# A two-layer decoder on one core: first rows loaded first, Mamba's weights laid out by a process, and another table of allowances for the order of work

## The chip, the cores and the metric

The kernel runs on one core of a Trainium2 chip. The core has four compute engines that run side by side, each through its own list of instructions in a fixed order: PE (TensorE, matrix products; PEld is its weight load), DVE (VectorE), ACT (ScalarE) and POOL (GpSimd). A fifth, SP (SyncE), issues all transfers between main memory and the core. The metric is the device time of one execution in microseconds (us), as the median of three runs.

## The reference, cut to what matters

The input `x` has 128 sequences of 64 rows of 128 numbers. Six layers follow one another, each added to `x`. All numbers are 32-bit floats unless said otherwise.

```python
x = x + mamba_block(layernorm(x))              # W_in, causal conv, scan over 64 steps, gate, W_out, then an MLP 128-512-128
x = x + pointer_attention(layernorm(x), ctx)   # each row looks at 3 rows of ctx named by an index; two softmaxes
x = x + bitlinear_ffn(layernorm(x))            # ternary weights, 8-bit activations, gelu, 128-512-128
x = x + causal_attention_twice(layernorm(x))   # 16 heads of 8; the context goes through a conv and becomes the next query
x = x + cross_attention(layernorm(x), ctx)     # 16 heads of 8, additive mask
x = x + moe(layernorm(x))                      # 8 experts 128-256-128, two best per row, all eight computed
# moe returns its own input as well: out = x_flat + sum_e cw[:, e] * (relu(x_flat @ W1[e] + b1[e]) @ W2[e] + b2[e])
```

In the Mamba block the input goes through `rmsnorm(., norm1_w)` and `W_in`; the time step is `softplus(... + dt_bias)`, the decay is `exp(-exp(A_log) * dt)`. The weights that multiply a normalized row (`norm1_w`, `norm2_w`, `norm_gate_w`) can be multiplied into the rows of `W_in`, `mlp_w1` and `W_out` once; the kernel does that.

## The kernel before, in words

The 128 sequences are worked in 16 groups of 8 (512 rows, held as 4 chunks of 128 rows). Each group passes through ten stages, named in `LAYERS`: prepare, project, recur, mlp (together the Mamba block), pointers, ternary, first, second (the two causal attentions), cross, experts. A stage takes one group at a time and seven groups are under way at once, since there are seven buffers for the rows (`x`). When the experts of a group are done, its rows are stored, its buffer is given back, and the rows of the group seven places later are loaded into it (`way`, L1718 to L1730).

What comes next on each engine is not decided on the chip. Each stage is written as a Python generator that says which engine it wants next and for how long (`yield V, 0.75`), or which token it needs (a buffer, a PSUM bank `"a"`, the four-bank tile `"s"`, its turn in a layer). The class `Turns` (L78) plays all generators against each other with these lengths before the program is built, and the order in which it serves them is the order of the instructions on PE, DVE, ACT and POOL. `dv`, `ac` and `po` (L369 to L376) are the lengths of elementwise work on DVE, ACT and POOL by the number of columns. Transfers on SP have no lengths there: a stage that needs one waits a fixed time (`yield None, 2.5` after the load of the rows), or none. The plan also halves PE's rate for a stretch of 3.413 us whose predecessor was less than 74% busy (`STRETCH`, `ENOUGH`).

Where several processes ask for one engine, the one that holds a scarce token goes first, and among equals the older one. The age is a tuple: the rank, then the time at which it asked plus the allowance of its layer (`age`, L142). A positive allowance makes a layer look younger, so it gives way. All processes have rank 0 but one: `ahead` (L1732), which turns the context rows of all groups into keys and values, has rank 1 and comes last always. The allowances are searched for while the program is built: `planned` (L228) tries 150 random changes of them, plays the plan with the instructions switched off (`Engine`, `Stand`), and keeps what ends earliest in the plan's own account.

The work ahead of the first group is not part of the plan. The parameter vectors are loaded and turned (L342 to L348), then `mamba` (L446) loads `W_in` (`win`), the conv weights, `W_out` (`wout`), `mlp_w1`, `mlp_w2` and the rest, and multiplies the norms into them on DVE (L454, L470, L472), each instruction in place in the lists as written. Only then does `way` issue the loads of the rows. A process `weights` (L1748) prepares the weights of the other layers among the work of the first groups.

Lines that the text below speaks of: L285 is every matrix product, L396 every transpose through PE, L398 the ACT copy behind it; L386 and L387 are the mean and variance of the rows on DVE, L365 and L366 the reciprocal root on POOL, L404 the centred rows `u` on POOL; L542 is the logarithm in prepare on ACT, L651 the last step of the decays on DVE; L1142 is the rounding of the hidden rows on POOL in the ternary layer; L1265 and L1267 are the maximum (`amx`, DVE) and its subtraction (POOL) in the cross attention; L1700 adds an expert's output to the rows on DVE.

## Time and profile before

| | |
|---|---|
| median of 3 runs | 2204.68 us (2203.23 to 2210.49) |
| profiled execution, its own time | 2200.66 us |
| its span, first to last instruction | 2198.8 us |
| mean clock granted to TensorE | 0.935 |
| PE busy | 1906.6 us, 87% of the span |
| DVE, ACT, POOL busy | 1474.3, 1163.1, 1005.9 us (67%, 53%, 46%) |
| DMA | 120.75 MB, mean 55 GB/s |

Busy times of PE are sums of matrix products as the profiler records them; a product takes longer where the granted clock is lower. "Idle before" a group of instructions is the time in which its engine had nothing running just before them, with the event that ended it, the releaser. A wait of an engine that is not the limit costs nothing by itself. The queries used are the page of the whole execution, the table of busy times by stretch, the list of waits by engine, the chain of work that ended last, and the timeline.

### The profile page before, as it was taken

The page shows a single profiled execution, that of the slowest core. Times are in us where ns is not written, and L with a number is a line of the kernel's source. Part 1 is how long each engine was busy: PE and PEld are TensorE (multiplying, and loading weights), DVE is VectorE, ACT ScalarE, POOL GpSimd, SP SyncE. Part 2 cuts the span into 40 slices and gives each one's busy share as a digit, 9 for nine tenths or more (in the row PEclk, how much of TensorE's full clock was granted, in tenths as well). Part 3 has the DMA queues.
Part 4 walks back from the last instruction along what each step waited for, and adds up shares of the span by engine and source line. Part 5 has one row for each costly group of instructions (what it writes and reads, how often), then busy time and mean ns, then how long its engine had stood idle before and what let it go on. Part 6 is the DMA issues. An engine that isn't in the chain of part 4 may idle for free.

```text
span 2198.8 us, 57057 instructions
## 1 busy us (share of the span) xinstructions
PE 1906.6 (87%) x23915; PEld 1352.6 (62%) x23920; DVE 1474.3 (67%) x3991; ACT 1163.1 (53%) x2134; POOL 1005.9 (46%) x1258
## 2 busy tenths in 40 slices
PE   3787678899998898989998989789988889898996
PEld 2555455566666566667666666566665666675664
DVE  2677777875576776767776876688586856745453
ACT  1555456655545654655554655556455545554442
POOL 1555755754426644363445462536453733523221
PEclk9888789999999999999999999889999999999998
DMA  6441212211112111021210201121101010101000
GB/s 179 160 151 56 73 40 79 80 50 35 38 63 81 64 52 59 25 68 38 86 35 21 97 33 56 55 83 38 45 18 61 14 41 2 35 7 41 26 6 6
DMA packets 87277, 120.75 MB, mean 55 GB/s; under 512 B 31622, under 2 KB 61292, under 8 KB 87020
## 3 DMA queue, kind: packets, MB, share of 16 engines
q1 hardware_dynamic: 87020, 117.10, 16.0%
q8 instruction: 188, 3.08, 0.6%
q14 instruction: 69, 0.57, 0.1%
HBM read 75.00 MB, written 42.07 MB: 53 GB/s over the span
## 4 chain that ended last, share of the span: by engine, by line
PE 52%; DVE 25%; POOL 9%; ACT 7%; DMA 3%; issue 3%; SPq 1%; DVEq 0%; POOLq 0%; ACTq 0%
PE psa L285 37%; PE pss L285 11%; PE psa L396 4%; POOL u L404 3%; DVE tops L1310 3%; DVE pT L1253 1%; DVE amx L1265 1%; DVE pT L609 1%; DVE st L386 1%; DMA x<-in_x 1%; DVE x L1700 1%; DVE sel L909 1%; DVE mv L387 1%; DVE s L916 1%; POOL r L1142 1%
## 5 line engine op out<-in xcount | busy, mean ns | idle before, releaser
L365 POOL TENSOR_SCALAR rsq<-mv 128x4 f32<-128x4 f32 x96 | 21.6, 225 | 538.9 <-DVE mv L387 532.2
L404 POOL TENSOR_SCALAR u<-x,mv,rstd 128x128 f32<-128x128 f32 x320 | 256.1, 811 | 23.2 <-PE psa L396 12.9
L285 PE MATMUL psa<-fT,moe_w 128*128 128x512 f32 x512 | 255.3, 615 | 10.2 <-DVE pT L651 3.7
L285 PEld LDWEIGHTS psa<-moe_w,hid 128*128 128x128 f32 x2048 | 244.4, 195 | 29.6 <-issue 19.8
L285 PE MATMUL psa<-moe_w,hid 128*128 128x128 f32 x2048 | 252.9, 279 | 4.1 <-ACT v_a L289 2.5
L1700 DVE SCALAR_TENSOR_TENSOR x<-psa,cw,x 128x128 f32<-128x128 f32 x512 | 144.0, 343 | 164.8 <-PE psa L285 164.8
L1678 ACT ACTIVATE hid<-psa,vcol 128x512 f32<-128x512 f32 x256 | 174.2, 688 | 150.3 <-PE psa L285 146.8
L1267 POOL TENSOR_TENSOR pT<-pT,amx 128x512 f32<-128x512 f32 x128 | 133.9, 1048 | 175.9 <-DVE amx L1265 151.6
L1343 ACT ACTIVATE pT<-pss 128x512 f32<-128x512 f32 x256 | 137.3, 604 | 104.4 <-PE pss L285 104.2
L1310 DVE TENSOR_REDUCE tops<-pss 128x32 f32<-128x2048 f32 x64 | 146.2, 2284 | 34.4 <-PE pss L285 34.2
L1142 POOL TENSOR_SCALAR r<-h 128x512 bf16<-128x512 f32 x64 | 98.3, 1544 | 143.6 <-DVE h L1140 106.7
L285 PEld LDWEIGHTS psa<-fT,moe_w 128*128 128x128 f32 x512 | 87.5, 192 | 83.8 <-issue 51.2
L285 PEld LDWEIGHTS pss<-km,qm 32*128 32x128 f32 x3072 | 103.1, 201 | 57.2 <-issue 39.8
L285 PE MATMUL pss<-km,qm 32*128 32x128 f32 x3072 | 122.5, 300 | 14.7 <-DVE pT L1253 8.6
L398 ACT COPY fT<-psa 128x512 f32<-128x512 f32 x112 | 65.8, 590 | 105.2 <-PE psa L396 105.0
L386 DVE BATCH_NORM_STATS2 st<-x 128x6 f32<-128x128 f32 x384 | 102.9, 268 | 24.4 <-DMA x<-in_x 23.8
L1387 DVE TENSOR_TENSOR fT<-psa,inv 128x256 f32<-128x256 f32 x96 | 40.2, 419 | 116.4 <-ACT inv L1385 114.2
L285 PE MATMUL psa<-pT,cst 128*32 128x256 f32 x1536 | 113.0, 404 | 3.8 <-DVE u L735 1.5
L1269 ACT ACTIVATE pT<-pT 128x512 f32<-128x512 f32 x128 | 79.8, 632 | 68.5 <-POOL pT L1267 68.0
L1383 ACT ACTIVATE inv<-psa 128x256 f32<-128x256 f32 x96 | 36.9, 384 | 120.5 <-PE psa L285 120.3
L396 PE MATMUL psa<-cst,u 128*128 128x128 f32 x384 | 72.9, 299 | 30.6 <-POOL u L404 22.9
L1253 DVE TENSOR_TENSOR pT<-pss,mask 128x512 f32<-128x512 f32 x128 | 87.3, 682 | 15.3 <-PE pss L285 15.2
(285 smaller groups left out, 4529.7 us busy)
## 6 DMA issues: line engine op xcount, KB each, us to landing
v_x<-v_x SPq DMA_DIRECT2D x32, 768.0 KB, 4.1
kT<-kT SPq DMA_DIRECT2D x32, 512.0 KB, 3.0
vo<-vo SPq DMA_DIRECT2D x32, 512.0 KB, 4.3
pT<-steps SPq DMA_DIRECT2D x64, 256.0 KB, 3.8
km<-km SPq DMA_DIRECT2D x32, 512.0 KB, 3.2
x<-in_x SPq DMA_DIRECT2D x16, 256.0 KB, 3.2
ctxT<-in_ctx SPq DMA_DIRECT2D x16, 256.0 KB, 2.7
mask<-in_mask_Bx1xSxS_ff SPq DMA_DIRECT2D x32, 128.0 KB, 2.8
```

Source lines behind the costliest of these rows:

```text
L285: T.matmul(o, lhsT=lhsT, rhs=rhs, start=start, stop=stop)
L386: V.bn_stats(st[:, c, :], X[:, c, :])
L396: T.transpose(pt[:, c * P : (c + 1) * P], part, by)
L404: G.tensor_scalar(u[:, c, :], X[:, c, :], mean(c), scale[:, c : c + 1], ALU.subtract, ALU.mult)
L1142: G.tensor_scalar(r2, h[:, c, :], -MAGIC, None, ALU.add)
L1253: V.tensor_tensor(sco, banks[:, r].rearrange("p (b h s) -> p b h s", b=4, s=S), mask[:, 4 * quad : 4 * quad + 4, :].unsqueeze(2).to_broadc ...
L1267: G.tensor_tensor(s3, s3, mx.unsqueeze(2).to_broadcast([P, 8, S]), ALU.subtract)
L1269: A.activation(sco, sco, AF.Exp)
L1310: V.tensor_reduce(mx[:, :, 0:8], banks.rearrange("p r (n s) -> p r n s", s=S), AX.X, ALU.max)
L1343: A.activation(pTs[r].rearrange("p b g q -> p (b g q)"), banks[:, r, :], AF.Exp)
L1678: A.activation(hid[:, b, :], ph, AF.Relu, bias=vec["moe_b1"][:, 2 * e + b : 2 * e + b + 1])
L1700: V.scalar_tensor_tensor(X[:, c, :], po_[:, c * P : (c + 1) * P], cw[:, c, e : e + 1], X[:, c, :], ALU.mult, ALU.add,)
```

## The change

The sum of all work stays the same: the same instructions of each kind on each engine, except that one load of an ACT table at the very start goes away. What changes is their order, in six ways.

1. The rows of group 0 are loaded right behind the constants, ahead of the parameter vectors and all weights.
2. What lays out Mamba's weights (multiplying the norms in, the decay constant, the identity for the scan) becomes a process of the plan, `setup`, with lengths. Two tokens, `win` and `wout`, hold prepare and recur back until it is done. The loads of the small parameters go ahead of `wout`, `mlp_w1` and `mlp_w2`.
3. The plan's length of POOL work becomes 0.22 + n/480 us for n columns (it was 0.1 + n/500), and the rounding of L1142 gets 1.55 us (it was 1.12).
4. The rank goes away. `ahead` is a process like the others with an allowance of 47.6 us.
5. The allowances are a table in the file in place of the search. The classes for playing the plan without instructions go away.
6. The small buffer `amx` has eight copies instead of four.

```diff
-    def layer(self, name):
-        self.running["allowance"] = self.allowances.get(name, 0.0)
+    def layer(self, name, group=None):
+        self.running["allowance"] = self.allowances.get(name, 0.0) + self.allowances.get((name, group), 0.0)
...
-        return process["rank"], process["time"] + process["allowance"], self.n
+        return process["time"] + process["allowance"], self.n
...
-def planned(layers, names, rounds=150):
...
+ALLOWANCES = {
+    "ahead": 47.6,
+    "mlp": 17.6,
+    "cross": -0.7,
+    "pointers": 12.3,
+    "ternary": -46.6,
+    "first": -6.5,
+    "second": 10.0,
+    "experts": 1.7,
+}
...
     def po(n):
-        return 0.1 + n / 500
+        return 0.22 + n / 480
...
         win = load("win", [P, 548], w["L0_attn_W_in"], mp)
-        V.tensor_scalar(win, win, vec["norm1_w"], None, ALU.mult)
+        dtb = broadcast(mp, "dt_bias", w["L0_attn_dt_bias"], 4)
+        alog = broadcast(mp, "A_log", w["L0_attn_A_log"], 4)
...
+        def setup():
+
+            yield None, 4.0
+            yield V, 1.2
+            V.tensor_scalar(win, win, vec["norm1_w"], None, ALU.mult)
+            for i in range(2):
+                V.tensor_copy(wbc[:, 32 * i : 32 * i + 16], win[:, 512 + 16 * i : 528 + 16 * i])
+            yield A, 0.2
+            A.activation(nega, alog, AF.Exp)
+            yield V, 0.8
+            V.tensor_scalar(nega, nega, -1.0, None, ALU.mult)
+            V.tensor_copy(eye4, ident.unsqueeze(1).to_broadcast([P, 4, P]))
+            turns.give("win")
+            yield None, 6.0
+            yield V, 0.5
+            for b in range(2):
+                V.tensor_scalar(wout[:, b, :], wout[:, b, :], vec["gate_w"][:, b : b + 1], None, ALU.mult)
+            yield V, dv(512)
+            V.tensor_scalar(w1, w1, vec["norm2_w"], None, ALU.mult)
+            turns.give("wout")
...
+            yield "win"
+            turns.give("win")
...
+            yield "wout"
+            turns.give("wout")
...
-                yield G, po(512)
+                yield G, 1.55
                 G.tensor_scalar(r2, h[:, c, :], -MAGIC, None, ALU.add)
...
-            mx = sm([P, 8], "amx", bufs=4)
+            mx = sm([P, 8], "amx", bufs=8)
...
-        xs[g] = wk([P, C, P], "x", bufs=BUFS["x"])
-        Q.dma_start(xs[g], tokens(xf, g))
+        if g:
+            xs[g] = wk([P, C, P], "x", bufs=BUFS["x"])
+            Q.dma_start(xs[g], tokens(xf, g))
...
+        turns.layer("ahead")
...
     def layers(allowances):
         stages.clear()
+        xs[0] = wk([P, C, P], "x", bufs=BUFS["x"])
+        Q.dma_start(xs[0], tokens(xf, 0))
+        vectors()
         turns.__init__(TOKENS, ("a", "s"), T, allowances)
         mamba(pools["weights"])
         A.preload_act_table_set(EXP_LN)
-        return turns.run([(0, way(g)) for g in range(NG)] + [(0, weights()), (1, ahead())])
...
+        turns.run([stages["setup"]()] + [way(g) for g in range(NG)] + [weights(), ahead()])
```

## The prediction

> **What bounds the kernel now.** I read the page first, then the table of stretches, then the waits of PE, POOL and DVE, the chain, and the timeline of the first 75 us.
>
> ```profile
> PE 1906.6 (87%) x23915; PEld 1352.6 (62%) x23920; DVE 1474.3 (67%) x3991; ACT 1163.1 (53%) x2134; POOL 1005.9 (46%) x1258
> ...
> PE 52%; DVE 25%; POOL 9%; ACT 7%; DMA 3%; issue 3%; SPq 1%; DVEq 0%; POOLq 0%; ACTq 0%
> ```
>
> PE is the limit, and 2198.8 - 1906.6 = 292.2 us of the span are PE's idle time. The instructions stay, so only this idle time, and the clock at which PE's work runs, can move. By stretch (columns: length, then PE, PEld, DVE, ACT and POOL busy, granted clock, DMA share, GB/s):
>
> ```profile
> 50.00:100.00 50.00, 38.71 (x227) 24.26 (x224) 35.52 (x92) 27.27 (x49) 19.61 (x28) 0.82 0.50 179
> 100.00:200.00 100.00, 82.14 (x463) 55.29 (x463) 66.06 (x192) 54.42 (x109) 58.60 (x85) 0.83 0.30 107
> 200.00:300.00 100.00, 71.94 (x458) 47.63 (x457) 80.12 (x204) 50.55 (x84) 66.09 (x84) 0.76 0.17 59
> 300.00:400.00 100.00, 83.84 (x1192) 57.13 (x1192) 79.51 (x192) 62.33 (x117) 54.35 (x65) 0.98 0.23 79
> 400.00:2000.00 1600.00, 1446.92 (x19384) 1035.89 (x19390) 1114.00 (x3004) 883.33 (x1621) 757.10 (x931) 0.95 0.14 48
> 2000.00:2150.00 150.00, 133.41 (x1964) 97.27 (x1964) 71.28 (x199) 66.71 (x127) 40.08 (x47) 0.97 0.04 13
> ```
>
> Idle time of PE: 36.8 us in the first 50, 11.3 in the next 50, 45.9 from 100 to 300, 153.1 from 400 to 2000 (9.6%), 16.6 from 2000 to 2150. No stretch is bad enough for one repair to give much; the long middle loses a tenth in small waits. These are PE's waits that the change could touch, and DVE's for the rows (us in total, times, longest):
>
> ```profile
> PE psa L396 <- POOL u L404: 22.9, 39, 4.8
> PE psa L434 <- DMA pT<-in_L_xattn_Wout: 16.8, 1, 16.8
> ...
> PE psa L396 <- DMA ctxT<-in_ctx: 12.5, 1, 12.5
> ...
> PE psa L396 <- POOL r L1142: 11.2, 11, 2.9
> ...
> PE psa L285 <- POOL km L708: 2.6, 3, 1.3
> ...
> DVE st L386 <- DMA x<-in_x: 23.8, 8, 7.3
> ```
>
> **The change part by part.** Since work stays and order moves, I read the instruction lists of both programs as built, and count the work between two places of a list by the durations of the rows of the trace.
>
> *First rows early, and setup: the opening, 0.* The rows of group 0 now land near 5 us instead of 15.7, and their `u` on POOL would be ready about 10 us earlier. But PE's list still opens with the pointers' weight products ahead of the transposes of `u`, and they wait until 23 us for `Wout`. The next stop stays as well. In ACT's list the order is, before and after, `fT`, the exponential, the copy of the context (L398), then the logarithm L542:
>
> ```profile
> 30.57 0.22 ACT L533 ACTIVATE e<-e 128x16 f32<-128x16 f32 x1 [3.18 <-DVE e L530]
> 44.47 0.58 ACT L398 COPY ctxT<-psa 128x512 f32<-128x512 f32 x1 [13.68 <-PE psa L396]
> 44.95 0.22 ACT L542 ACTIVATE lw<-wp 128x16 f32<-128x16 f32 x1
> ```
>
> The context load is issued at 37.78 behind 55 other transfers on SP. The same 55 stand ahead of it afterwards, so group 0 is held until about 44.5 us either way. That covers the early rows, the table load that goes (1.28 us in ACT's idle 10.8 us), and the eight parameter loads and `win` that SP now issues one transfer (0.4 us) later. DVE meets the products for `wout` and `mlp_w1` behind the pointers' index work, near 27 us, when these loads have long landed (before, at 9.7 and 10.7 us); what is queued behind them there waits for nothing new. If this cover went, those 10 us would be the price of either sign; I take 0, bounds -2 and +2.
>
> *The second group: -5.* DVE's list before has the scans of group 0 and a weight copy (58.69 to 63.7) ahead of the last two statistics of group 1. POOL sat until then, and PE waited for its `u`:
>
> ```profile
> 58.69 4.56 DVE L609 TENSOR_TENSOR_SCAN pT<-pT,eye 128x512 f32<-128x512 f32 x4
> ...
> 64.71 0.19 POOL L365 TENSOR_SCALAR rsq<-mv 128x4 f32<-128x4 f32 x1 [39.07 <-DVE mv L387]
> ```
>
> After, all four statistics stand ahead of the scans: POOL starts about 4.56 + 0.64 = 5.2 us earlier. Late next is the gate of group 0: its two products come behind three context products of about 1.1 us in PE's list, but PE was idle for some 8 us between 59 and 72 us. I take -5; bounds 0 (the gate takes it all) and -8.
>
> *POOL's lengths: -14.* Before, the plan gave L1142 1.12 us (the row has 1.544), a 512-wide sum 1.12 (1.27 to 1.34), a 256-wide product 0.61 (0.78), a 128-wide sum 0.36 (0.50). Now it gives 1.55, 1.29, 0.75, 0.49. Per group the plan was short by about 4 x 0.42 + 5 x 0.17 + 4 x 0.17 + 4 x 0.14 = 3.8 us. Instructions that the plan thinks ready too early put PE in a wait: 22.9 + 11.2 + 2.6 = 36.7 us above. The L404 waits come only partly from this, as that row (0.811) was already planned at 0.83. I take all of L1142 and the rest of L708, -14; bounds 0 and -37. No release of PE can be credited twice: in the stretch from 300 on the single waits are 1 to 2 us and some of what they free is lost again to the next one.
>
> *The table and the lost rank: the reload of rows, +6.* DVE's statistics of group g+7 cannot start until the rows of group g are stored and the new ones have landed:
>
> ```profile
> 538.62 3.31 DMA out<-x
> 541.94 3.92 DMA x<-in_x
> ```
>
> That is 7.2 us; the plan counts 2.5. What matters is how much DVE work the list has between the last L1700 of one and the first L386 of the other. By the rows, the nine gaps before are 0, 3.4, 4.4, 6.2, 15.1, 2.5, 9.6, 4.2 and 2.2 us: short of 7.2 by 27.5 in all, of which the trace has 21.6 (23.8 less the 2.2 of the first rows). After, they are 2.5, 0.4, 3.5, 3.0, 2.8, 4.8, 0.8, 0.7 and 1.8: short by 44.5, and at the same ratio 35 us of wait, 13 more. Queued behind the waiting L386 is everything else on DVE, which PE then misses. The chain before runs over these transfers, so some of it counts, but DVE has 33% of room: I take half, +6; bounds 0 and +13.
>
> *The table: the end, -3.* Counted by rows, the PE work in the list behind the last group's second convolution grows from 124 to 153 us: the last group is further on, and more work of others stands beside it. From 2000 to 2150 PE idles 16.6 us where the middle's 9.6% would be 14.3; -3, bounds 0 and -6. The last 33 us are the last group's experts alone, in both lists.
>
> *The table: all other waits, 0.* The order in the middle is dealt anew. I compared the PE work between a producer and its consumer for 25 hand-overs (scores to maxima, maxima to transposes, output to next norm and so on): the sum by which it falls short of the latency in between is 51 us before and 56 after. So the lists give no reason for a gain. How much a new deal may move is read from eight stretches of 200 us between 400 and 2000, which have the same mix: PE busy from 175.7 to 184.6, spread about 3, clocks 0.91 to 0.97. Over nine stretches that gives some 9 us of idle time and about as much of clock: bounds -20 and +20.
>
> *`amx`: 0.* POOL waits 151.6 us for DVE's L1265; DVE does not wait for POOL there (L1265 has 0.5 us of idle time, behind DVE itself). Bounds 0 and -1.
>
> *The clock.* Two stretches with nearly the same PE busy time, 100 to 200 and 300 to 400, got 0.83 and 0.98: 15 us of full rate per 100 us, not explained by idle time alone. The Trainium skill (TensorE: Matmul & The Clock Gate, "What's actually happening") says that the clock halves after an idle window of about 3.4 us and recovers after a busy one. In this trace that is not the whole of it: from 100 to 200 us, at 0.83, no single wait of PE is above 2.7 us. By the page, removing waits of 1 to 3 us would bring no clock; by the rows a denser opening may bring up to 15 us. I leave it in the range.
>
> *The sum.* 0 - 5 - 14 + 6 - 3 + 0 = -16 on the profiled execution's 2200.66 us: 2184.7. The median of the runs lies 4.0 above that execution, so 2188.7, say 2189 (-0.7%). Differences under 0.3% (6.6 us) can't be told from no change.
>
> **The rivals.**
>
> *A. The reload of rows becomes the wait that counts: slower.* Place: L386 on DVE, nine times. Price: all 13 us reach PE, and each of the nine stops costs a stretch of 3.413 us at half rate (1.7 us each, 15 in all), and POOL's lengths bring nothing: 13 + 15 - 5 - 3 = +20, 2225 us. For it: the chain goes out -> in -> L386 at 538 us. Against it: DVE is 67% busy. It decides as soon as more than 8 us of the extra cost go uncovered, while POOL's lengths bring nothing.
>
> *B. The new plan is better in the crowded opening too.* All 37 us of waits for POOL go, the clock from 100 to 300 rises to the mean of 0.93 (10 + 17 = 27 us, of which I count 20): -37 - 20 - 5 - 3 + 6 = -59, 2146 us. For it: POOL is busiest just there (58.6 and 66.1 of 100). Against it: the comparison of hand-overs.
>
> *C. A deal as good as the last.* Gains at POOL are given back elsewhere, 2198 to 2211 us.
>
> **How the numbers follow.** The forecast's own range is 2165 to 2198, with a chance of 0.46; B 0.12, C 0.14, A and other bad deals 0.28. Faster 0.58, same 0.14, slower 0.28. Eight in ten: from B's 2146 to 2226, just past A.
>
> **What would show it.** Right: PE's waits for L1142 under 5 us; POOL's first L365 of group 1 near 60 us; L542 still near 45; DVE's wait for `x` near 35 us; PE idle about 276 us. Wrong: new PE waits for DVE's L1310 or L682 that outweigh POOL's, or a mean clock further than 0.01 from 0.935.

## The result and the profile after

The changed kernel took 2237.37 us (median of 4 runs, 2230.05 to 2244.66), the kernel before 2207.59 us in the same comparison (4 runs, 2203.23 to 2212.84). The ratio is 1.0134, with a 95% interval from 1.0087 to 1.0181. The change made the kernel slower by 30 us; the forecast was 2189 us, and its range ended at 2226. The profiled execution after took 2244.66 us, with a span of 2242.8 us and a mean granted clock of 0.928 (before: 2200.66, 2198.8, 0.935).

The lines of the changed kernel are mostly 8 to 30 lower than those of the kernel before: L285 is now L255, L396 and L398 are L371 and L373, L404 is L379, L365 is L340, L386 is L361, L542 is L532, L1142 is L1134, L1253 is L1245, L1648 is L1640, L1310 is L1302, L682 is L672, L973 is L965, L708 is L698.

The first part and the chain of the page after:

```profile
PE 1931.6 (86%) x23916; PEld 1365.6 (61%) x23920; DVE 1496.1 (67%) x3991; ACT 1161.4 (52%) x2133; POOL 1032.3 (46%) x1258
...
PE 52%; DVE 29%; POOL 6%; ACT 6%; issue 3%; DMA 3%; SPq 1%; POOLq 0%; DVEq 0%; ACTq 0%
```

PE's idle time is 2242.8 - 1931.6 = 311.2 us, 19.0 more than before, and the same products took 25.0 us more, at a lower clock. DVE's share of the chain rose from 25 to 29%, POOL's fell from 9 to 6%.

The table of stretches after (length; then PE, PEld, DVE, ACT, POOL busy, granted clock, DMA share, GB/s). The last two lines are the same distances from the end as the lines from 2000 to 2150 and from 2150 to 2198.80 of before:

```profile
0.00:400.00 400.00, 289.51 (x2592) 193.18 (x2593) 264.06 (x707) 202.04 (x369) 213.05 (x273) 0.88 0.32 105
400.00:2000.00 1600.00, 1425.63 (x18778) 1014.65 (x18778) 1123.22 (x2965) 861.05 (x1586) 771.50 (x931) 0.94 0.14 47
...
2044.00:2194.00 150.00, 137.75 (x1858) 101.17 (x1850) 75.75 (x219) 65.13 (x121) 38.79 (x46) 0.98 0.05 14
2194.00:2242.80 48.80, 36.42 (x184) 25.58 (x184) 14.45 (x57) 11.81 (x18) 3.51 (x4) 0.81 0.02 6
```

The first 400 us of before, and its last 48.80:

```profile
0.00:400.00 400.00, 289.87 (x2392) 193.81 (x2394) 274.54 (x733) 201.24 (x368) 206.58 (x279) 0.87 0.32 105
2150.00:2198.80 48.80, 36.42 (x182) 25.65 (x182) 14.46 (x57) 11.81 (x18) 2.14 (x3) 0.81 0.02 6
```

PE's busy time in the first 400 us is as before (289.51 against 289.87). The last 198.8 us idle a little less (24.6 us against 29.0). The middle is where the time came from: between 400 us and the last 198.8 us lie 1600 us before and 1644 after. In these 1644 us PE is busy for 1931.61 - 289.51 - 137.75 - 36.42 = 1467.9, against 1446.9: so of the 44 us, 23 are idle time and 21 are the same kind of products running slower. (Stretches of equal length don't hold exactly equal work, so this splits the time by place and not by cause.)

PE's waits after (total us, times, longest):

```profile
PE psa L371 <- POOL u L379: 28.6, 40, 5.0
PE psa L1648 <- DVE cw L1640: 26.4, 12, 5.1
PE pss L255 <- DVE pT L1245: 26.3, 10, 7.0
PE psa L371 <- POOL r L1134: 19.4, 12, 5.6
PE psa L371 <- DVE att L965: 18.0, 3, 9.1
...
PE psa L371 <- POOL km L698: 6.8, 1, 6.8
```

Every one of these was smaller before, when the list read (of the DVE lines, in the order of the lines above):

```profile
PE psa L1656 <- DVE cw L1648: 11.8, 5, 5.2
...
PE pss L285 <- DVE pT L1253: 13.7, 9, 6.6
...
PE psa L396 <- DVE att L973: 6.9, 3, 5.0
```

These three waits for DVE grew by 38.3 us together; the three for POOL that the forecast meant to shorten grew from 36.7 to 55.7 (28.6 + 19.4 + 6.8, and 0.9 of PE's L255 for `km`, the place where it waited before). Other waits shrank, so the net is 19. No new mechanism stands out in these lists; many hand-overs that fitted before now fit a little worse.

### The profile page after: what moved, and what is told of

It reads as the page before. It is cut to its first block, busy times and chain, and to the rows that moved or that the text cites. A ratio compares the mean times of both kernels' runs of the same rounds, so it can differ in the third digit from the quotient of the medians.

```text
span 2242.8 us, 57011 instructions
## 1 busy us (share of the span) xinstructions
PE 1931.6 (86%) x23916; PEld 1365.6 (61%) x23920; DVE 1496.1 (67%) x3991; ACT 1161.4 (52%) x2133; POOL 1032.3 (46%) x1258
## 4 chain that ended last, share of the span: by engine, by line
PE 52%; DVE 29%; POOL 6%; ACT 6%; issue 3%; DMA 3%; SPq 1%; POOLq 0%; DVEq 0%; ACTq 0%
PE psa L255 36%; PE pss L255 11%; PE psa L371 4%; POOL u L379 3%; DVE tops L1302 2%; DVE pT L1245 2%; DVE amx L1257 2%; DVE x L1692 2%; DMA x<-in_x 1%; DVE st L361 1%; DVE mv L362 1%; DVE s L908 1%; DVE qm L564 1%; DVE sel L901 1%; DVE pT L599 1%
## 5 line engine op out<-in xcount | busy, mean ns | idle before, releaser
L379 POOL TENSOR_SCALAR u<-x,mv,rstd 128x128 f32<-128x128 f32 x320 | 264.9, 839 | 31.2 <-PE psa L371 21.8
L255 PEld LDWEIGHTS psa<-moe_w,hid 128*128 128x128 f32 x2048 | 242.5, 194 | 25.8 <-issue 14.4
L255 PE MATMUL psa<-fT,moe_w 128*128 128x512 f32 x512 | 254.4, 616 | 2.3 <-ACT hid L1670 1.5
L255 PE MATMUL psa<-moe_w,hid 128*128 128x128 f32 x2048 | 252.7, 279 | 1.8 <-DVE x L1692 1.1
L340 POOL TENSOR_SCALAR rsq<-mv 128x4 f32<-128x4 f32 x96 | 26.8, 279 | 463.1 <-DVE mv L362 445.9
L1302 DVE TENSOR_REDUCE tops<-pss 128x32 f32<-128x2048 f32 x64 | 146.1, 2283 | 39.4 <-PE pss L255 39.1
L1134 POOL TENSOR_SCALAR r<-h 128x512 bf16<-128x512 f32 x64 | 98.8, 1555 | 157.5 <-DVE h L1132 157.5
L255 PE MATMUL pss<-km,qm 32*128 32x128 f32 x3072 | 123.5, 302 | 24.3 <-DVE pT L1245 23.5
L255 PEld LDWEIGHTS pss<-km,qm 32*128 32x128 f32 x3072 | 104.0, 203 | 64.0 <-issue 51.0
L255 PEld LDWEIGHTS psa<-fT,moe_w 128*128 128x128 f32 x512 | 89.3, 195 | 76.7 <-issue 53.0
L255 PE MATMUL psa<-pT,cst 128*32 128x256 f32 x1536 | 116.9, 396 | 6.2 <-DVE hid L1652 3.4
L361 DVE BATCH_NORM_STATS2 st<-x 128x6 f32<-128x128 f32 x384 | 103.2, 269 | 26.2 <-DMA x<-in_x 25.5
L694 POOL TENSOR_TENSOR qm<-qm,km 128x256 f32<-128x256 f32 x64 | 50.7, 793 | 148.4 <-DVE qm L689 148.4
L373 ACT COPY fT<-psa 128x512 f32<-128x512 f32 x112 | 65.2, 586 | 73.1 <-PE psa L371 72.5
L371 PE MATMUL psa<-cst,u 128*128 128x128 f32 x384 | 72.7, 297 | 31.9 <-POOL u L379 28.6
```

The lines of the kernel that those rows point to most:

```text
L255: T.matmul(o, lhsT=lhsT, rhs=rhs, start=start, stop=stop)
L361: V.bn_stats(st[:, c, :], X[:, c, :])
L371: T.transpose(pt[:, c * P : (c + 1) * P], part, by)
L373: A.copy(o, pt)
L379: G.tensor_scalar(u[:, c, :], X[:, c, :], mean(c), scale[:, c : c + 1], ALU.subtract, ALU.mult)
L1134: G.tensor_scalar(r2, h[:, c, :], -MAGIC, None, ALU.add)
```

## The experiments

Two theories were held against the prediction's own steps. *The parts:* early rows and setup, POOL's lengths, and the new table each have a price of their own, and one of them is bad. *The draw:* each table of allowances fits one plan. The table before was picked by a search on exactly its plan, so any edit to the plan, whatever it is for, loses that fit and lands among ordinary orders. All kernels below compute the same as the two kernels; only the order of the lists and of some transfers differs. Ratios are to the kernel before, run beside each set.

### The change taken apart

**table_alone**: the kernel before with the new table, and no rank.

```diff
-        layers(best)
+        layers(ALLOWANCES)          # the changed kernel's table
...
+        turns.layer("ahead")
...
-        return turns.run([(0, way(g)) for g in range(NG)] + [(0, weights()), (1, ahead())])
+        return turns.run([(0, way(g)) for g in range(NG)] + [(0, weights()), (0, ahead())])
```

> The kernel before with only the new table (ahead at 47.6 in place of the rank); start, POOL lengths and amx as before. Theory T, the table and the lost rank cost the time: about +30 us on the kernel before (2230 to 2245). Theory P, the longer POOL lengths cost it: within 7 us of before. Theory D, every part only deals the order anew and the times scatter by some 20 us without adding up: anything from 2185 to 2250, and the parts alone will not sum to the +30 us.

Measured: 2350.52 us, ratio 1.0670 [1.0639, 1.0701]; clock 0.897. The two largest lines of its list of PE's waits (us in all, times, longest):

```profile
PE psa L368 <- POOL u L376: 53.7, 61, 6.7
PE psa L1287 <- DVE tops L1282: 30.3, 19, 3.7
```

**all_but_table**: the changed kernel with the table that the kernel before had found, and `ahead` last.

```diff
 ALLOWANCES = {
-    "ahead": 47.6, "mlp": 17.6, "cross": -0.7, "pointers": 12.3,
-    "ternary": -46.6, "first": -6.5, "second": 10.0, "experts": 1.7,
+    "project": -12.5, "pointers": 6.2, "recur": -14.3, "mlp": -5.2, "cross": -19.2,
+    "experts": -5.6, "prepare": 6.7, "ternary": -14.3, "first": -0.8, "ahead": 1000000.0,
 }
```

> The changed kernel with the table that the kernel before found by its search, and ahead always last (an allowance of a million us, which ranks it behind everything); new start, new POOL lengths, eight amx. Theory T: back to the time before, within 7 us of 2206. Theory P: stays near 2237. Theory D: anywhere between 2185 and 2250.

Measured: 2253.13 us, 1.0221 [1.0183, 1.0259].

**pool_lengths_alone**: the kernel before, its own table, with POOL's lengths of the change.

```diff
-        return 0.1 + n / 500
+        return 0.22 + n / 480
...
-                yield G, po(512)
+                yield G, 1.55
                 G.tensor_scalar(r2, h[:, c, :], -MAGIC, None, ALU.add)
```

> The kernel before, its own table kept fixed, with only the new POOL lengths in the plan (0.22 + n/480 and 1.55). Prediction's own step: 14 us faster than before, PE's waits for L1142 under 5 us. Theory T: no more than 7 us from before. Theory P: +20 to +30 us. Theory D: off by 10 to 30 us to either side, with PE's waits for POOL not smaller.

Measured: 2235.23 us, 1.0143 [1.0113, 1.0173].

**start_alone**: as all_but_table, with the lengths of before as well; what is left is the early rows, setup as a process, and `amx`.

```diff
-        return 0.22 + n / 480
+        return 0.1 + n / 500
...
-                yield G, 1.55
+                yield G, po(512)
```

> The changed kernel's start (rows of group 0 first, setup as a process, eight amx) with the table, the rank and the POOL lengths of before. Prediction's own step: the start itself is worth 0 to -7 us, the logarithm of group 0 still near 45 us. Theory T and theory P: within 7 us of before. Theory D: the tokens and the new process deal the order anew from the first microseconds on, so off by 10 to 30 us to either side although nothing at the start is worth that.

Measured: 2255.64 us, 1.0240 [1.0207, 1.0273].

The parts don't add. The new table alone costs 150 us, POOL's lengths alone 35, the start alone 55, start and lengths together 53; and all of them together 30. A table that costs 150 us in the plan of before brings some 16 to 19 (2253 to 2237, or 1.0221 to 1.0134) in the changed plan. That is what the draw says, and a theory of priced parts can't. But the scatter is larger than even the draw (theory D in the texts above) was expected to give: table_alone lies 100 us beyond its range, start_alone and pool_lengths_alone are off by 55 and 35 us where 10 to 30 were expected, and all of them to the slow side.

### The fit of a table

**nudge**: the kernel before with its own table, one allowance half a microsecond larger.

```diff
-    "mlp": -5.2,
+    "mlp": -4.7,
```

> The kernel before, its own table kept, with one allowance moved by half a microsecond (mlp from -5.2 to -4.7). Nothing else. Theory D, the time is the luck of the fit between one table and one plan, which any change loses: 30 to 100 us slower than before, with more waits of PE of every kind. Theory S, the new start and lengths have a cost of their own, and theory T, this table does: within 7 us of before.

Measured: 2269.12 us, 1.0291 [1.0250, 1.0333]. DVE's list is the same, instruction for instruction, for its first 987 entries, about a quarter of it and some 530 us. From there the lists part. The table of stretches of nudge:

```profile
0.00:500.00 500.00, 381.29 (x3950) 262.65 (x3951) 344.09 (x922) 262.81 (x488) 266.51 (x349) 0.89 0.29 95
500.00:1000.00 500.00, 460.67 (x5919) 325.32 (x5919) 357.14 (x955) 280.35 (x516) 242.32 (x294) 0.97 0.16 52
1000.00:1500.00 500.00, 447.50 (x5524) 316.46 (x5523) 345.36 (x941) 273.50 (x504) 235.36 (x297) 0.93 0.17 56
1500.00:2000.00 500.00, 428.76 (x5706) 307.31 (x5704) 325.35 (x874) 245.65 (x438) 212.46 (x253) 0.91 0.09 29
```

and of the kernel before:

```profile
0.00:500.00 500.00, 381.02 (x3964) 259.65 (x3966) 345.82 (x926) 262.59 (x488) 265.83 (x349) 0.89 0.29 95
500.00:1000.00 500.00, 449.30 (x5847) 324.12 (x5848) 336.89 (x926) 274.63 (x504) 240.84 (x301) 0.95 0.17 55
1000.00:1500.00 500.00, 456.37 (x5836) 323.09 (x5834) 364.13 (x975) 281.39 (x523) 236.55 (x303) 0.95 0.17 56
1500.00:2000.00 500.00, 450.10 (x6130) 322.85 (x6135) 341.69 (x910) 265.97 (x475) 220.46 (x258) 0.95 0.10 30
```

Up to 500 us the two are alike. Just after it nudge is even the denser one; from 1000 to 2000 its PE is idle for 123.7 us against 93.5, and the clock goes down to 0.91. From 2000 us to the end it is idle for 50.0 us, against 29.0 before. In all PE is idle for 39.6 us more, and its work takes 26.3 us more. No length, no transfer and no stage was changed: 66 us is what another deal of the same work, middle and end, can cost.

**no_table**: the kernel before without allowances.

```diff
-        layers(best)
+        layers({})
```

> The kernel before with an empty table (all allowances zero; rank kept). It tells what the search of before was worth, and where an unfitted plan lies. Theory D: 2235 to 2310, as slow as or slower than the changed kernel, in line with the parts run alone (2235 to 2350). Theories S and T give no figure, but if it lies within 10 us of before, D falls.

Measured: 2270.32 us, 1.0289 [1.0253, 1.0325]. So the searched table is worth 67 us, and half a microsecond in one entry loses all of it.

**searched_again**: the changed kernel with the table that the search of the kernel before (150 tries) finds on the changed plan.

```diff
 ALLOWANCES = {
-    "ahead": 47.6, "mlp": 17.6, "cross": -0.7, "pointers": 12.3,
-    "ternary": -46.6, "first": -6.5, "second": 10.0, "experts": 1.7,
+    "ahead": 1000000.0, "project": -28.3, "ternary": -1.1, "pointers": -9.0, "recur": -5.1,
 }
```

> The changed kernel (start, POOL lengths, amx) with a table found for it by the search of before: 150 random changes, same chance, ahead last. Theory T: back to about 2206. Theory S: about 2237 or above. Theory D: a draw of the same kind as the others, 2205 to 2260, not set by what is kept of the change.

Measured: 2249.07 us, 1.0194 [1.0164, 1.0225]. The same search gave 2208 on the one plan and 2249 on the other: the table of before was a good draw as well as a searched one.

**long_search** (the changed kernel) and **before_long_search** (the kernel before), each with a table from some 3,500 tries in place of 150.

```diff
 # the changed kernel
 ALLOWANCES = {
-    "ahead": 47.6, "mlp": 17.6, "cross": -0.7, "pointers": 12.3,
-    "ternary": -46.6, "first": -6.5, "second": 10.0, "experts": 1.7,
+    "ahead": 77.1, "mlp": 37.8, "cross": -0.7, "pointers": 12.3, "ternary": -333.7, "first": -294.7,
+    "second": 14.7, "experts": 1.9, "recur": 4.9, "project": 12.1, "prepare": 0.4,
 }
...
 # the kernel before
+    "project": -0.5, "pointers": -5.4, "recur": -8.4, "mlp": 12.8, "cross": -217.7,
+    "experts": -5.4, "prepare": 19.4, "ternary": -14.0, "first": -6.4,
```

> The changed kernel with a table found for it by some 3600 random changes in place of 150; all else as in the changed kernel, ahead not last either. Theory S: stays near 2237 or above 2225. Theory T: cannot tell, the table is new again. Theory D: a better fit is found by more draws, below 2215 and perhaps below before, with PE's waits for POOL and DVE down.

> The kernel before (old start, old POOL lengths, ahead last by rank) with a table found by some 3600 random changes in place of 150. Theory D: the search is what counts, so it lands where the changed kernel with the long search did, 2180 to 2200. Theory that the change's parts have a worth of their own (rows first, true POOL lengths): 2200 or above, 10 us or more behind the 2189 of the changed kernel with the long search.

Measured: 2189.41 us, 0.9930 [0.9907, 0.9953], and 2169.50 us, 0.9845 [0.9811, 0.9879], the second 10 us under the lowest time that was expected of it. PE's waits for `r` are 24.7 us in long_search, more than in any of the slower kernels: waits for POOL don't decide.

### Has the change a worth of its own?

One long table each leaves open whether 20 us between the two kernels are the change or the draw. So each got a second one, and POOL's lengths a run under a long table of their own.

**before_long_2**, **changed_long_2** and **pool_lengths_long** (the kernel before with POOL's lengths as in pool_lengths_alone):

```diff
 # before_long_2
+    "project": -9.7, "pointers": 6.5, "recur": -20.3, "mlp": 14.6, "cross": -19.3,
+    "experts": 1.7, "prepare": 18.9, "ternary": -14.3, "first": -13.6, "second": 21.7,
...
 # changed_long_2
+    "ahead": 48.6, "mlp": 31.6, "cross": -0.7, "pointers": 2.2, "ternary": -63.8, "first": 7.9,
+    "second": 10.0, "experts": 1.7, "recur": -3.1, "prepare": 0.0, "project": 0.0,
...
 # pool_lengths_long
+    "project": -9.2, "pointers": 7.6, "recur": -14.4, "mlp": -1.8, "cross": -16.4,
+    "experts": -5.6, "prepare": 20.7, "ternary": -18.7, "first": -14.0, "second": 2.9,
```

> The kernel before with another table from a long search (before_long_search took 2169.5 us with the first one). If which kernel a long search starts from has a worth of its own, this lies within 8 us of 2169.5. If the draw decides, it may lie anywhere between 2150 and 2200, on either side of the changed kernel's two.

> The changed kernel with another table from a long search (long_search took 2189.4 us with the first one). If the change costs some 20 us of its own beside any good table, this lies at 2181 to 2197 and above both tables of the kernel before. If the draw decides: between 2150 and 2200.

> The kernel before with POOL's lengths as traced and a table from a long search. If the lengths are worth the 14 us that the prediction gave them, once the table fits them, this lies near 2155 (2169.5 less 14). If they are worth nothing beside the draw: between 2150 and 2200, with PE's waits for POOL not under the 52 us of long_search by more than a few us.

Measured: before_long_2 2187.21 us, 0.9928 [0.9901, 0.9955]; changed_long_2 2174.84 us, 0.9885 [0.9840, 0.9929]; pool_lengths_long 2175.27 us, 0.9884 [0.9847, 0.9921]. Two tables of one kernel lie 18 us and 15 us apart, and the pairs (2169.5 and 2187.2 before, 2189.4 and 2174.8 after) lie inside each other. No worth of the change shows, of either sign, and none of POOL's lengths; with two draws each (one for the lengths alone), a worth smaller than that spread could not show. PE's waits for POOL are another matter: of the nine kernels with a table from a long search, below too, the two with the old lengths have 53.4 and 56.5 us of them, the seven with the new lengths 36.3 to 52.3. So true lengths may shorten these waits, but the times don't follow them.

### The opening

**context_first**: the changed kernel, lists of all compute engines unchanged, with the first load of the context issued right behind Mamba's weights instead of behind all other weights.

```diff
     def layers(allowances):
...
+        first[:] = [wk([P, C, P], "ctxT", bufs=2)]
+        Q.dma_start(first[0], tokens(cf, 0))
         turns.run([stages["setup"]()] + [way(g) for g in range(NG)] + [weights(), ahead()])
...
-        following = loaded(0)
+        following = first[0]
```

> The changed kernel; only the load of the first group's context rows is issued right behind Mamba's weights in place of behind the other layers' weights. The lists of PE, DVE, ACT and POOL stay as they are, instruction for instruction. Prediction's step on the opening: the logarithm of group 0 stood behind this load until about 44.5 us and hid the early rows; now it runs near 32 us, the cover is gone, and some 10 us of the opening come free. If the opening is on the path: 2225 to 2230 us. If the opening is hidden by later work anyway: within 4 us of 2237.

Measured: 2228.05 us, 1.0110 [1.0080, 1.0141]; the span fell from 2242.8 to 2231.5. The logarithm L532 went from 46.12 to 35.65 us, the first L340 of the second group from 62.01 to 52.00. **long_context_first** is the same edit on long_search:

> The same move of the first context load, with the table of the long search (2189 us). If the opening is on the path: near 2179, the fastest so far. If not: 2185 to 2193.

Measured: 2176.12 us, 0.9886 [0.9853, 0.9919], against 0.9930 for long_search; the span fell from 2185.6 to 2169.0. The medians fell by 9.3 and 13.3 us, the ratios by 0.0024 and 0.0044 (5 and 10 us), and each pair of intervals overlaps. In the two pairs of profiled executions the gain lasts: the first store of finished rows comes 16.8 and 11.2 us earlier, the 15th of the 16 still 13.0 and 16.7. So these 10 us at the start are likely worth 5 to 13 at the end; one profiled execution of each doesn't make it certain.

### A plan nearer to the trace

**waits_as_traced**: the changed kernel with two of the plan's fixed waits set nearer to the trace, the context issued ahead of the other layers' weights (with a planned wait of 0.5), and a long table.

```diff
         def prepare(g):
...
-            yield None, 2.5
+            yield None, 6.9 if g > 6 else 2.5
...
     def ahead():
-        yield "laid"
         following = loaded(0)
-        yield None, 2.5
+        yield "laid"
+        yield None, 0.5
...
     def weights():
-        yield None, 6.0
+        yield None, 19.0
...
-        turns.run([stages["setup"]()] + [way(g) for g in range(NG)] + [weights(), ahead()])
+        turns.run([stages["setup"]()] + [way(g) for g in range(NG)] + [ahead(), weights()])
...
+    "ahead": 34.1, "ternary": -14.4, "recur": -2.7, "mlp": 14.6, "project": 2.5,
+    "cross": -96.1, "first": 2.4, "prepare": 20.2, "second": 5.0,
```

> The changed kernel with the first context load ahead of all other layers' weights, and two waits of the plan set to what the trace shows: 6.9 us in place of 2.5 for rows that are loaded into a buffer just stored, 19 in place of 6 for the other layers' weights; then a long search of its own (some 3500 changes). If a plan nearer to the trace gives better orders: below 2180, DVE's waits for x under 10 us. Theory D alone: 2180 to 2200, as any long search.

Measured: 2134.35 us, 0.9683 [0.9649, 0.9717]. **waits_as_traced_2** has another long table:

```diff
+    "ahead": 36.1, "mlp": 8.9, "cross": -5.9, "pointers": 12.3, "ternary": -122.9, "first": 7.2,
+    "second": 11.4, "experts": 6.3, "prepare": 24.5, "project": 20.2, "recur": -29.7,
```

> waits_as_traced (2134.35 us) with another table from a long search. If the plan's waits for the transfers and the early context have a worth of their own, this lies at 2120 to 2150, under every other table of both kernels, and DVE's wait for the rows stays under 12 us. If 2134 was a lucky draw: between 2150 and 2200.

Measured: 2137.97 us, 0.9715 [0.9672, 0.9758]. Both beat the kernel before by 3%, and every other order here by 24 us or more. With a spread of 15 to 18 us between draws, this is more than a draw. Then one part each, with a long table of its own: **context_and_weights_waits** puts the reload's wait back to 2.5, **reload_wait** is the changed kernel with the 6.9 alone.

```diff
 # context_and_weights_waits, against waits_as_traced
-            yield None, 6.9 if g > 6 else 2.5
+            yield None, 2.5
...
+    "ahead": 48.1, "mlp": 23.9, "cross": -15.6, "pointers": 11.4, "ternary": -12.8, "first": -17.0,
+    "second": 7.0, "experts": 1.7, "recur": -8.7, "prepare": 0.4,
...
 # reload_wait, against the changed kernel
-            yield None, 2.5
+            yield None, 6.9 if g > 6 else 2.5
...
+    "ahead": 60.8, "mlp": 34.4, "cross": -3.8, "pointers": 0.6, "ternary": -31.0, "first": 1.6,
+    "second": 3.7, "experts": 1.7, "project": 12.3, "recur": 0.0,
```

> waits_as_traced without the reload's wait (6.9 back to 2.5) and a table from a long search of its own. If the gain of waits_as_traced over the other long tables (about 45 us) is the opening (PE waits 28 us less there for transfers), this lies at 2134 to 2155. If it is the reload's wait, this lies at 2165 to 2190 and DVE waits 15 us or more for the rows.

> The changed kernel with the reload of the rows planned at 6.9 us in place of 2.5 and a table from a long search of its own; the opening as changed. If the reload's wait brings the gain: 2134 to 2150. If the opening brings it: 2165 to 2190 (as the other long tables), with DVE's wait for the rows under 12 us all the same and PE's 35 us of waits for transfers still there.

Measured: 2163.55 us, 0.9824 [0.9798, 0.9850], and 2162.48 us, 0.9820 [0.9791, 0.9849]. Neither expectation of a single cause held: each alone lies between, some 20 us under the mean of the changed kernel's two long tables (2182.1), both together 46. Against the spread between draws of 15 to 18 us, each single gain, of one draw, is likely at best; only the two together stand clear of it.

I had expected the gain of the context and weights at the opening itself, and that was mostly wrong. In waits_as_traced the first group's logarithm runs at 20 us, as ACT's timeline there has it (start, duration, engine, line, operation; in brackets the idle time before and its releaser):

```profile
20.26 0.21 ACT L533 ACTIVATE lw<-wp 128x16 f32<-128x16 f32 x1 [0.24 <-DVE wp L529]
```

PE's timeline shows that it then waits for another thing, the pointers' index on DVE, until 52.63 us:

```profile
52.63 0.36 PE L846 MATMUL psa<-cst,pT 64*128 64x64 f32 x1 [21.77 <-DVE pT L842]
```

That index stands on DVE behind the scans of group 0, and these waited for a transfer. Their input goes out to main memory and comes back; it was ready at 22.8 us, but SP issued its store only at 40.01, behind the weights of the other layers. From SP's timeline and DVE's:

```profile
40.01 0.33 SPq L554 DMA_DIRECT2D steps<-arows  x1
47.90 4.57 DVE L600 TENSOR_TENSOR_SCAN pT<-pT,eye 128x512 f32<-128x512 f32 x4 [15.94 <-DMA pT<-steps]
```

So the stop moved from one transfer behind the weights to the next: the scans wait 14.31 us for `steps` in waits_as_traced_2 and 15.64 in context_and_weights_waits. No run tries this store ahead of the weights.

By 400 us little is gained. The table of stretches of waits_as_traced has hardly more PE work in the first 400 us than the changed kernel (290.73 us against 289.51, at a clock of 0.86 against 0.88), though 13.7 us more of DVE's, and 65 us more of PE's in the next 1600:

```profile
0.00:400.00 400.00, 290.73 (x2397) 195.66 (x2397) 277.73 (x750) 199.14 (x368) 215.89 (x285) 0.86 0.33 108
400.00:2000.00 1600.00, 1490.51 (x20481) 1070.69 (x20483) 1146.05 (x3067) 916.77 (x1689) 791.69 (x946) 0.97 0.15 47
```

waits_as_traced_2 has 299.71 us of PE in its first 400 us, context_and_weights_waits 288.86.

### All orders in one table

PE's idle time from 400 to 2000 us (1600 less PE's busy time there) goes with the time of the whole, whichever part was changed (medians of different sets; the kernel before had 2200.5 to 2207.6 in them; context_first and long_context_first have the orders of the changed kernel and of long_search and are left out):

| kernel | median us | PE idle, 400 to 2000 | PE waits for POOL | clock |
|---|---|---|---|---|
| table_alone | 2350.5 | 208.3 | 78.9 | 0.897 |
| no_table | 2270.3 | 177.4 | 66.4 | 0.926 |
| nudge | 2269.1 | 173.5 | 43.1 | 0.922 |
| start_alone | 2255.6 | 159.7 | 55.6 | 0.924 |
| all_but_table | 2253.1 | 159.4 | 41.5 | 0.924 |
| searched_again | 2249.1 | 173.4 | 53.6 | 0.930 |
| the changed kernel | 2237.4 | 174.4 | 57.0 | 0.928 |
| pool_lengths_alone | 2235.2 | 160.0 | 43.3 | 0.933 |
| the kernel before | 2207.6 | 153.1 | 36.9 | 0.935 |
| long_search | 2189.4 | 142.9 | 52.3 | 0.935 |
| before_long_2 | 2187.2 | 148.3 | 56.5 | 0.934 |
| pool_lengths_long | 2175.3 | 135.5 | 39.0 | 0.925 |
| changed_long_2 | 2174.8 | 135.0 | 36.3 | 0.940 |
| before_long_search | 2169.5 | 128.1 | 53.4 | 0.935 |
| context_and_weights_waits | 2163.6 | 123.9 | 38.8 | 0.934 |
| reload_wait | 2162.5 | 119.0 | 47.3 | 0.938 |
| waits_as_traced_2 | 2138.0 | 108.8 | 40.1 | 0.935 |
| waits_as_traced | 2134.4 | 109.5 | 42.9 | 0.943 |

The waits for POOL (summed over PE's list of waits by releaser) don't order the times: 53.4 us of them stand in a kernel of 2169.5, 36.9 in one of 2207.6. The middle's idle time does, with few exceptions, and most of it is made of short waits for all engines: after, PE's whole list has 238 waits, of 303 us together. DVE's waits for the rows don't order the times either: nudge, at 2269.1 us, has 9.9 us of them, changed_long_2, at 2174.8, 23.7.

## Why the prediction was wrong

*The step that failed: "The table: all other waits, 0", with its bounds of -20 and +20.* This step and those on POOL's lengths and the reload lie in the middle, between 400 us and the last 198.8, with -8 together; the runs put it at +44. The reload's part of that is small, and the lengths cost nothing that shows under a table of their own (both below). Two faults are in the step on the table. The bounds came from the spread of eight stretches within one order, 3 us each. But these stretches share one plan; the spread that counts is that between orders, and it reaches from 2134 to 2350. The four orders that keep the searched numbers (nudge all but one of them) and edit something around them (pool_lengths_alone, start_alone, all_but_table, nudge) are all slower, by 35 to 66 us. And 0 was the wrong centre. The order before had been selected out of 150 on its own plan, and a new deal isn't drawn around a selected one but around what is usual: no_table stands 67 us above it. The changed kernel, at 2237, is one of the usual ones: the six other orders with no table, with the searched one out of its fit, or with one from 150 tries on the changed plan lie from 2235 to 2270, and table_alone at 2350. The prediction took the order before as a sample of itself.

*The comparison of 25 hand-overs (51 against 56 us short)* gave "no reason for a gain", and was used as no reason for a loss. It was counted by durations, and the waits that grew most, 38.3 us for DVE's `cw`, `pT` and `att`, are 25 waits of up to 5.1, 7.0 and 9.1 us. Why the count over the lists missed them, no run shows.

*POOL's lengths, -14: not found.* The waits for `u`, `r` and `km` grew from 36.7 to 55.7 us where the step had them fall; with the lengths alone (pool_lengths_alone) they are 40.2, and `r` has 12.6, not under 5. A length that matches the row can only move a wait where POOL's own duration was the late link. POOL's group of L1142, now L1134, shows for what it waited itself, before and after (columns: count, then busy time and mean ns, then idle time before with its releasers):

```profile
L1142 POOL TENSOR_SCALAR r<-h 128x512 bf16<-128x512 f32 x64 | 98.3, 1544 | 143.6 <-DVE h L1140 106.7 <-ACT hid L1678 22.5 <-ACT inv L1383 5.3
...
L1134 POOL TENSOR_SCALAR r<-h 128x512 bf16<-128x512 f32 x64 | 98.8, 1555 | 157.5 <-DVE h L1132 157.5
```

POOL stood idle for DVE's `h` for 157.5 us after and 106.7 before: the rows come later from DVE. That this, and not POOL's length, is why PE waits for `r` is argued and not tried. Under a long table the lengths bring no gain that can be told from the draw (2175.3, between 2169.5 and 2187.2).

*The second group, -5: 0.* POOL did start earlier, though by 2.7 us instead of 5.2: the statistics stand ahead of the scans, but the last of the four is behind conv steps (L564, 56.7 to 61.0) that began 3.7 us later than the same six before. What was won was lost at once, in a way that I hadn't counted. POOL's timeline after:

```profile
62.01 1.01 POOL L340 TENSOR_SCALAR rsq<-mv 128x4 f32<-128x4 f32 x1 [44.85 <-DVE mv L362]
63.10 1.88 POOL L341 TENSOR_TENSOR r<-rsq,cst 128x4 f32<-128x4 f32 x1
65.06 0.20 POOL L492 TENSOR_TENSOR rs<-mv,r 128x4 f32<-128x4 f32 x1
65.33 1.04 POOL L493 TENSOR_TENSOR rs<-rs,r 128x4 f32<-128x4 f32 x1
66.46 0.19 POOL L340 TENSOR_SCALAR rsq<-rs 128x4 f32<-128x4 f32 x1
...
68.14 3.14 POOL L379 TENSOR_SCALAR u<-x,mv,rs 128x128 f32<-128x128 f32 x4
```

and DVE's of the same time:

```profile
61.84 4.54 DVE L599 TENSOR_TENSOR_SCAN pT<-pT,eye 128x512 f32<-128x512 f32 x4
66.30 0.65 DVE L1407 COPY pT<-pT 128x384 f32<-128x384 f32 x1
```

Beside the scans L340, L341 and L493 on POOL take 1.01, 1.88 and 1.04 us; before, the same three took 0.19, 1.04 and 0.31 with no scan beside them, and behind the scans L340 takes 0.19 again. (L492, which ends with a scan, has its usual 0.20.) The `u` began at 68.14 us, against 68.54 before: 0.4 us are left of the 2.7. In the bounds of the step (0), for a reason that it didn't name.

*The reload of rows, +6: too large.* DVE waits 25.5 us for the rows in place of 35, 4 more than the 21.6 of before, where 13 were forecast:

```profile
DVE st L361 <- DMA x<-in_x: 25.5, 9, 6.0
```

The term that was mis-sized is the 7.2 us from the store to the first statistic. It was read at the reload of 538.62 us, the longest of the seven at which DVE waited before: at the other six it went on 5.1 to 6.6 us after the store was issued. After, the nine take 4.9 to 6.7 us, with a mean of 5.4; with each one's own time the gaps of the list are short by 28.1 us in place of 44.5, near the 25.5 of the trace. At the step's own half this is +2. Rival A (2225 us) came near in time, but its place was not where the time went. The reload mattered in another sense: planned at 6.9 us instead of 2.5, DVE's wait is 5.6 us (reload_wait), though before_long_2, with the 2.5, has 8.1.

*The opening, 0: right.* L532 stands at 46.12 us, just behind the copy of the context, whose load is issued at 38.92 us (behind 58 transfers in both kernels by SP's timeline, not 55):

```profile
45.64 0.59 ACT L373 COPY ctxT<-psa 128x512 f32<-128x512 f32 x1 [13.15 <-PE psa L371]
46.12 0.22 ACT L532 ACTIVATE lw<-wp 128x16 f32<-128x16 f32 x1
```

The prediction named the cover of "those 10 us", and context_first took it away: the ratio went from 1.0134 to 1.0110, and the profiled span fell by 11 us.

*The end, -3: right in size.* The last 198.8 us have 4.3 us less of idle time, on no more than one execution each. *`amx`, 0*, wasn't tried alone. *The clock*: 0.928 is within the 0.01 that was allowed, and 0.007 of it still goes with 25 us more of PE's busy time. Of the marks for a right one, L542 near 45 us and POOL's L365 near 60 (62.0) came; PE's waits for L1142 (19.4 us, not under 5), DVE's wait for `x` and PE's idle time (311 us, not 276) did not. The marks set for a wrong prediction were not met either: it was not DVE's L1310 or L682 that outweighed POOL's waits (`tops` and `xdt` fell from 45.0 us to 33.9 in PE's list), but other hand-overs.

On the clock, over these 18 orders of the same work it goes from 0.897 (table_alone, 208.3 us idle in the middle) to 0.943 (waits_as_traced, 109.5 us), though loosely: pool_lengths_long has 0.925 with 135.5 us. So an order that fits better tends to gain twice, in idle time and in clock, and the forecast's -16 counted the first alone. The Trainium skill (TensorE: Matmul & The Clock Gate, "What's actually happening") ties half rate to idle windows of some 3.4 us; the longest waits of the list after, at 5 to 9 us, fit that, but no run here tells which waits cost the clock. The prediction went further when it said that by the page the removal of waits of 1 to 3 us would bring no clock: the section doesn't say that shorter waits are free, and the row of 100 to 200 us, at 0.83 with no wait above 2.7 us, speaks against it.

What stays open: why an earlier context and later weights make the middle better, when context_and_weights_waits has gained nothing by 400 us (288.86 us of PE); how closely the plan's own end, by which the search picks, follows the measured time, which no run records; and whether the change has a worth of its own under the spread between draws.

## What to carry to other kernels

An order that was picked by a search is the best of its draws by the plan, and any edit to what the search saw, however right, should be expected to lose that fit first: price it as "searched order against ordinary order" (here 35 to 66 us of 2200), not as 0 plus the edit. Compare two plans only with each searched as long, and with more than one draw each; the spread between draws (15 to 18 us here) is the resolution. What paid here was to search longer (2169 to 2189 us for both kernels) and to bring the plan's waits nearer to the trace (the reload of rows at 6.9 us, not 2.5, where the traces have 4.9 to 7.3, and the weights at 19, not 6), with the context loaded earlier: 2134 us, 3.2% under the kernel before. And read a latency that goes into a sum at every place where it occurs, not at the one that stands out.

## What the runs showed of the hardware

DVE's scans held POOL up. Small POOL instructions (128x4) that take 0.19 to 0.20 us alone took 1.01 to 1.04 us while DVE ran scans of 128x512 (four in 4.54 us, some 1.13 us each), and a reciprocal root of 1.04 us took 1.88. If the four scans share their time equally, they end at 62.98, 64.11, 65.25 and 66.38 us; POOL's L340, L492 and L493 end at 63.02, 65.26 and 66.37. The scans lost nothing by it: they took 4.56 us before, where POOL stood idle. POOL's timeline of context_first has the same 10 us earlier, again beside the scans (52.71 to 57.28 us there):

```profile
54.01 1.04 POOL L493 TENSOR_TENSOR rs<-rs,r 128x4 f32<-128x4 f32 x1
55.14 1.02 POOL L340 TENSOR_SCALAR rsq<-rs 128x4 f32<-128x4 f32 x1
56.24 1.84 POOL L341 TENSOR_TENSOR rs<-rsq,cst 128x4 f32<-128x4 f32 x1
58.16 0.20 POOL L495 TENSOR_TENSOR rs<-rs,r 128x4 f32<-128x4 f32 x1
```

The last line starts after the scans and takes 0.20 us again. The Trainium skill (SBUF — State Buffer, "Who interferes with whom") tells of a port that the two engines share and that one holds for itself while an instruction with two SBUF inputs runs; the scans have two inputs, and the rows agree with it. So a statistic moved ahead of a scan on DVE may gain less on POOL than the lists say.

The second finding is the size of what order does: the same work on the same engines (but for one table load at the start) took from 2134 to 2350 us by the order of instructions and transfers, and the sum of PE's busy times ran from 1890.9 us (waits_as_traced, at a clock of 0.943) to 1978.8 us (table_alone, at 0.897).
